# A two-layer graph network on one core: ScalarE writes the own term of six of 24 slot tiles into PSUM, and the order of tiles, engines and PSUM buffers is laid out anew

## The chip, the core and the metric

The kernel runs on one core of a Trainium2 chip. The core has TensorE (matrix products, written PE in the profile, with PEld for the loading of its weights), VectorE (DVE), ScalarE (ACT), GpSimd (POOL) and SyncE (SP), whose queue issues nearly all DMA transfers here. Products land in PSUM, a memory of eight banks of 2 KB per partition; everything else lies in SBUF. The metric is the device time of one execution in microseconds (us).

## The reference, cut to what matters

There are 128 graphs of 128 nodes with 64 features, and two layers that each add to x. The first layer is the costly one: for every node j and each of its neighbours k it applies a ReLU to 192 hidden values, and adds these up over the neighbours.

```python
# layer 0, B = N = 128, F = O = 64, H = 192
h    = maximum(layernorm(x), 0)
mask = (adj > 0)
W1a, W1b = W1[:F], W1[F:]
hid  = relu((h @ W1a)[:, :, None] + (h[:, :, None] - h[:, None, :]) @ W1b + b1)
hm   = einsum('bjkh,bjk->bjh', hid, mask)
x    = x + hm @ W2 + mask.sum(-1)[..., None] * b2
# layer 1
h    = maximum(layernorm(x), 0)
x    = x + einsum('bnm,bmf->bnf', adj, h) @ W.T
```

The hidden value of the pair (j, k) is ReLU(a_j - c_k): one term that belongs to the node j itself, the *own term*, and one that belongs to its neighbour k. A node has some 16 neighbours, so the kernel doesn't form all 128 pairs of a node.

## The kernel before, in words

The 128 graphs are worked on in 32 groups of four. The neighbours of a node are taken by quarters of 32 nodes; in each quarter the first six neighbours of every node get a *slot*. A one-hot matrix S (slot, node j) picks the neighbour's value from the table `k3` by a matmul. A neighbour that finds no slot in its quarter goes through a second, smaller path (tiles `ov`, `R`, `S2`, `px`, `X`, `pe`).

**A tile** (class `Job`) holds one graph and half of its nodes (64), and two of the quarters, `qp`: 2 x 6 slots x 64 nodes = 768 columns in two PSUM banks. There are 16 tiles of kind 0 in a group (the first 128 hidden values) and 8 of kind 1 (the other 64 hidden values of two graphs together), 24 in all, written t0 to t23 below in the order in which the group works on them. `fill` writes a tile by TensorE: for each quarter one matmul of 384 columns with S picks the neighbours (profile: `g<-S,k`), then four matmuls of 192 columns with a repeated identity, `id3`, add the own term (`g<-id,k`). In kind 1 each of these is two matmuls of half the width. The values in `k3` are split into three bf16 parts that are stacked over 96 rows, so that one product adds all three. `drain` empties the tile: kind 0 by one VectorE reduction of absolute values (`hm<-g`), since ReLU(v) = (v + |v|)/2 and the plain sum comes from elsewhere; kind 1 by a ScalarE ReLU (`T<-g`) and a tree of GpSimd additions.

**The tables of the next group** are made while a group's tiles run. `pre_proj` projects (`pp`) into PSUM; ScalarE rounds this to a first bf16 part (`ca<-pp`), VectorE takes the remainder (`rest`), ScalarE rounds a second part (`ca<-rest`), GpSimd forms the third. `pre_stack` then copies the parts by twelve SyncE transfers into `k3` (profile: `k<-ca`), four quarters for each part, part by part. Beside this, `pre_rank` and `pre_slots` make S by six VectorE comparisons (`S<-qs`), and twelve SyncE transfers spread it over three copies for each quarter (`S<-S`). SyncE's queue thus issues in each group, in this order: the twelve of S, the twelve of `k`, the store of a result, and the loads of `x` and `adj`.

**The order** is written out by hand: `ORDER` lists the tiles, and `PLAN` says after which tile which step of which group is issued; steps of the next group have 1, of the group after that 2, of the one before -1. Each engine executes in this order. `ORDER0`/`PLAN0` and `ORDERL` are for the first and the last group. PSUM is three buffers of two banks (`gtile`, for tiles and `pp`) and two of one bank (`mtile`, for everything else), taken in turn.

**The e term** is the part of the result that depends on a node alone; ScalarE scales it out of `pp` in four instructions (`e<-pp,dn`), and GpSimd adds x to it (`e<-e,x`).

Every engine instruction goes through a helper, so that the profile shows lines L181 (matmul), L184 (transpose) and L198 (the other engines) for nearly everything; the tile names tell them apart.

Of the kernel before, what the change touches and what calls it, by code (L numbers as in the profile page):

```python
# [150 lines left out]
def kernel(  # L151
# [34 lines left out]
    class Engine:  # L186


        held = True
# [38 lines left out]
    with ExitStack() as main:  # L228
# [5 lines left out]
        ps_g = main.enter_context(tc.tile_pool(name="ps_g", bufs=3, space=PSUM))  # L234
        ps_m = main.enter_context(tc.tile_pool(name="ps_m", bufs=2, space=PSUM))

        def gtile(name):
            return ps_g.tile([P, 2, 512], F32, tag="g", name=name)

        def mtile(name):  # L240
            return ps_m.tile([P, 512], F32, tag="m", name=name)
# [130 lines left out]
        def weights_d():  # L372
            pl = mtile("pl")
            tp(pl[:, 0:P], wl1, ident)
            vec.tensor_copy(wl1t, pl[:, 0:P])
# [53 lines left out]
        def pre_stats(g):  # L429
            d = groups[g]  # L430
            d["mv"] = norm_a(d["x"], f"a{g}")
# [9 lines left out]
        def norm1(g, bs):  # L441
            d = groups[g]
            for b in bs:
                normed(d["h"][:, b % 2, b // 2, :], d["x"], d["scales"], b)
# [9 lines left out]
        def norm2(g, bs):  # L454
            d = groups[g]
            for b in bs:
                normed(d["h2"][:, b, :], d["x1"], d["scales"], b)
# [12 lines left out]
        def pre_adj(g):  # L470
            d = groups[g]
            pt = mtile(f"pt{g}")
            for b in range(G):
                tp(pt[:, b * N : (b + 1) * N], d["adj"][:, b, :], ident)
            d["adjT"] = grp.tile([P, G, N], F32, tag="adjT", name=f"adjT{g}", bufs=3)
            if g == 0:
                pre_norm(0)
            act.activation(
                d["adjT"].rearrange("k b j -> k (b j)"), pt, AF.Copy
            )  # L480
            if g < 2:
                return
            pre_mask(g)

        def pre_mask(g):
            d = groups[g]
            d["maskT"] = grp.tile([P, G, N], BF16, tag="maskT", name=f"maskT{g}", bufs=3)
            vec.tensor_scalar(d["maskT"], d["adjT"], 0.0, -1.0, ALU.is_gt, ALU.mult)
            if "mv" not in d:
                pre_stats(g)  # L490
# [7 lines left out]
        def pre_rank(g):  # L498
            d = groups[g]
            pq = mtile(f"pq{g}")  # L500
            mm(
                pq, triq, d["maskT"].rearrange("k b j -> k (b j)"), start=True, stop=True
            )
            d["qs"] = grp.tile([P, G, N], BF16, tag="qs", name=f"qs{g}")
            qf = d["qs"].rearrange("k b j -> k (b j)")
            act.activation(qf, pq, AF.Copy)

            d["ov"] = grp.tile([P, G, N], BF16, tag="ov", name=f"ov{g}")
            vec.tensor_scalar(d["ov"], d["qs"], float(D) + BIG, None, ALU.is_ge)

        def pre_slots(g, first, last):

            d = groups[g]
            if first == 0:
                d["S"] = one.tile([P, D, G * N], BF16, tag="S", name=f"S{g}")
            for i in range(first, last):
                vec.tensor_scalar(
                    d["S"][:, i], d["qs"].rearrange("k b j -> k (b j)"),
                    float(i) + BIG, None, ALU.is_equal,
                )  # L520
            if last < D:
                return
# [32 lines left out]
        def pre_hT(g):  # L555
            d = groups[g]
            ph = mtile(f"ph{g}")
            for r in range(2):
# [4 lines left out]
                )  # L563
            d["hT"] = tmp.tile([P, 2, N], F32, tag="hT", name=f"hT{g}", bufs=1)
            act.activation(
                d["hT"].rearrange("p r n -> p (r n)"), ph[:, 0 : 2 * N], AF.Copy
            )

        def pre_count(g):
            d = groups[g]  # L570

            pd = mtile(f"pd{g}")
            for b in range(G):
# [5 lines left out]
                )  # L579
            d["dn"] = grp.tile([P, 2, G], F32, tag="dn", name=f"dn{g}")  # L580
# [14 lines left out]
        def pre_proj(g, r, between=None):  # L595

            d = groups[g]
            if r == 0:

                d["ca"] = grp.tile([P, 3, 2, G, H], BF16, tag="ca", name=f"ca{g}")  # L600

# [3 lines left out]
            pp = gtile(f"pp{g}_{r}")  # L605
# [8 lines left out]
            for p in range(2):  # L614
# [5 lines left out]
            x = pp[:, :, 0 : 2 * H].rearrange("n p (t u) -> n p t u", t=2)  # L620
            parts = [
                d["ca"][:, i].rearrange("n t (p r) u -> n r p t u", p=2)[:, r] for i in range(3)
            ]
            act.activation(parts[0], x, AF.Copy)
            rest = tmp.tile([P, 2, 2, H], F32, tag="rest", name=f"rest{g}_{r}")

            def zs():
                for p in range(2):
                    b = 2 * p + r
                    for to, us, f in (  # L630
                        (d["z"][:, b], slice(0, C0), AF.Abs),
                        (d["z1"][:, r, p], slice(C0, H), AF.Relu),
                    ):
                        act.activation(to, x[:, p, 1, us], f, scale=d["ns"][:, b : b + 1])


            def es():
                for p in range(2):
                    b = 2 * p + r
                    act.activation(  # L640
                        d["e"][:, b], pp[:, p, 2 * H : 2 * H + O], AF.Copy,
                        scale=d["dn"][:, 0, b : b + 1],
                    )

            def second():
                act.activation(parts[1], rest, AF.Copy)

            def third(*engines):
                for t, engine in enumerate(engines):
                    engine.tensor_tensor(  # L650
                        parts[2][:, :, t], rest[:, :, t], parts[1][:, :, t], ALU.subtract
                    )

            def add_x():
                pool.tensor_tensor(d["e"], d["e"], d["x"], ALU.add)

            def residual():
                vec.tensor_tensor(rest, x, parts[0], ALU.subtract)

            return residual, zs, es, second, third, add_x  # L660

        def project(g, r):
            d = groups[g]
            d["steps", r] = pre_proj(g, r)
            d["steps", r][1]()
            d["steps", r][2]()
            if r == 1:
                d["steps", r][5]()

        def project_rest(g, r):  # L670
            groups[g]["steps", r][0]()

        def project_parts(g, r):
            steps = groups[g].pop(("steps", r))
            steps[3]()
            steps[4](pool, pool)

        def pre_stack(g):
# [13 lines left out]
        def pre_edge_a(g):  # L692
            d = groups[g]
            pv = mtile(f"pv{g}")
            mm(pv[:, 0:G], upb, d["nb"], start=True, stop=True)
            mm(pv[:, G : 2 * G], oneb, d["nb"], start=True, stop=True)
            vec.tensor_tensor(ovf, ovf, pv[:, G : 2 * G], ALU.max)

# [4 lines left out]
        def edge_abs(g):  # L703
            d = groups[g]
            d["et"] = tmp.tile([P, G, E], F32, tag="et", name=f"et{g}", bufs=1)
            for b in range(G):
                act.activation(d["et"][:, b, :], iov, AF.Abs, bias=d["mid"][:, b : b + 1])

        def pre_place(g):

            d = groups[g]
            pj = mtile(f"pj{g}")
# [8 lines left out]
            )  # L721
            d["qj"] = tmp.tile([P, G, N], BF16, tag="qj", name=f"qj{g}", bufs=1)
            act.activation(d["qj"].rearrange("j b k -> j (b k)"), pj, AF.Copy)
# [12 lines left out]
        def pre_edge_c(g):  # L736
            d = groups[g]
            pr = mtile(f"prt{g}")
            for b in range(G):
                mm(  # L740
                    pr[:, b * N : (b + 1) * N], d["R"][:, b, :], identb, start=True, stop=True
                )
            d["RT"] = grp.tile([P, G, N], F32, tag="RT", name=f"RT{g}")
            act.activation(d["RT"].rearrange("e b j -> e (b j)"), pr, AF.Copy, scale=-1.0)

        def pre_edge_d(g):
            d = groups[g]
            pg = mtile(f"pgq{g}")
            for b in range(G):
# [3 lines left out]
                )  # L753
            d["S2"] = grp.tile([P, G, E], BF16, tag="S2", name=f"S2{g}")
            vec.tensor_tensor(
                d["S2"], pg.rearrange("k (b e) -> k b e", b=G), bc(ioe, G, 1), ALU.is_equal
            )

        def edge_x(g, r):
            d = groups[g]  # L760
            if r == 0:
                d["X"] = grp.tile([P, G, H], F32, tag="X", name=f"X{g}", bufs=1)
            px = mtile(f"px{g}_{r}")
            for p in range(2):
                b = 2 * p + r
                for t, one_hot in enumerate(("S2", "R")):
                    for i in range(3):
# [3 lines left out]
                        )  # L771
            pxv = px[:, 0 : 2 * H].rearrange("e (p u) -> e p u", p=2)
# [12 lines left out]
        def edge_sum(g):  # L785

            d = groups[g]
            ph = mtile(f"pe0{g}")
            for b in range(G):
# [5 lines left out]
                for i in range(3):  # L795
# [3 lines left out]
                    )  # L799
            d["u0"] = tmp.tile([P, G, N], F32, tag="u0", name=f"u0{g}", bufs=1)  # L800
# [4 lines left out]
        def edge_sum1(g):  # L805
            d = groups[g]
            ph = d["pe1"] = mtile(f"pe1{g}")
# [12 lines left out]
        def edge_sum2(g):  # L820
# [8 lines left out]
        def post0(g):  # L829
            d = groups[g]  # L830
            py = d["py"] = mtile(f"py{g}")
# [11 lines left out]
        def post1(g):  # L843
# [4 lines left out]
            )  # L848
            d["mv"] = norm_a(d["x1"], f"b{g}")

        def post3(g):
            d = groups[g]
            pg = mtile(f"pga{g}")
# [243 lines left out]
```

## Time and profile before

| | |
|---|---|
| median of 3 runs | 963.09 us (962.8 to 963.93) |
| the profiled execution | 964.39 us, of which 962.6 us from the first to the last instruction (the span) |
| mean granted TensorE clock | 0.994 |
| busy in the span | PE 931.3 us, DVE 770.5, POOL 739.2, ACT 685.8 |
| DMA | 129.93 MB in 88296 packets; queue 1 took 58.3% of 16 engines' span |

"Busy" counts an instruction from its start to its end; consecutive instructions of an engine overlap, so what an instruction costs its engine is the distance to the start of the next one, which the timeline shows. In groups of instructions, `out<-in` names the tiles, with the numbers of buffers left out: `S<-S` is the transfer from the one-hot matrix to its copies.

### The profile page before, as it was taken

The numbers are of one execution on the slowest core, as the hardware profiler recorded it, in microseconds if no ns is written. First come the engines' busy times: TensorE is split into PE (matmuls) and PEld (weight loads), VectorE is DVE, ScalarE is ACT, GpSimd is POOL, SyncE is SP. The second block draws the span as 40 slices with busy tenths as digits, with TensorE's granted clock in tenths as the row PEclk, the third lists the DMA queues.
The fourth block names the chain that finished last, engine by engine and source line by source line (L and its number), as shares of the span: only waits on it lengthen the run. The fifth ranks groups of instructions, "written<-read, shape, count | busy, mean of one in ns | idle before, by whom it ended". The sixth has DMA issues, their size and how long they took to land.

```text
span 962.6 us, 27044 instructions
## 1 busy us (share of the span) xinstructions
PE 931.3 (97%) x10135; PEld 715.1 (74%) x10136; DVE 770.5 (80%) x1880; ACT 685.8 (71%) x1700; POOL 739.2 (77%) x1130
## 2 busy tenths in 40 slices
PE   6899999999999999999999999999999999999996
PEld 2677777777777777777777777777777777777774
DVE  6787878887878887878887878887878888878864
ACT  4857787767787767787767787667787667787652
POOL 1488787778787778787778787778887778887793
PEclk9999999999999999999999999999999999999998
DMA  4555676655576655676655576655676655676510
GB/s 101 127 126 128 142 165 146 147 130 127 142 171 140 142 134 127 142 170 141 146 130 128 140 171 140 142 133 123 146 163 144 148 129 129 142 172 140 125 46 14
DMA packets 88296, 129.93 MB, mean 135 GB/s; under 512 B 47200, under 2 KB 63968, under 8 KB 88160
## 3 DMA queue, kind: packets, MB, share of 16 engines
q1 hardware_dynamic: 87584, 127.98, 58.3%
q8 instruction: 82, 1.34, 0.6%
q14 instruction: 54, 0.44, 0.1%
q10 hardware_dynamic: 576, 0.16, 0.1%
HBM read 13.01 MB, written 4.19 MB: 18 GB/s over the span
## 4 chain that ended last, share of the span: by engine, by line
PE 68%; DVE 15%; ACT 10%; DMA 4%; POOL 1%; issue 1%; SPq 0%; POOLq 0%; ACTq 0%; DVEq 0%
PE g L181 39%; PE pe L181 9%; PE px L181 6%; DVE hm L198 5%; ACT z L198 3%; ACT ca L198 3%; DVE rest L198 3%; DMA S<-S 3%; PE pp L181 2%; DVE stb L198 2%; PE po L181 2%; ACT e L198 1%; DVE u L198 1%; PE pga L181 1%; PE ph L184 1%; PE pj L181 1%
## 5 line engine op out<-in xcount | busy, mean ns | idle before, releaser
L198 POOL TENSOR_TENSOR T<-T 128x192 f32<-128x192 f32 (+2 forms) x768 | 522.6, 687 | 119.1 <-ACT T L198 79.2
L198 DVE TENSOR_REDUCE hm<-g 128x64 f32<-128x768 f32 x512 | 477.1, 948 | 100.9 <-PE g L181 96.1
L181 PEld LDWEIGHTS <-k 96*128 96x128 bf16 (+1 forms) x6144 | 413.1, 104 | 173.7 <-issue 55.4
L181 PE MATMUL g<-S,k 96*128 96x384 bf16 (+1 forms) x2048 | 381.7, 329 | 12.3 <-DVE hm L198 10.2
L181 PE MATMUL g<-id,k 96*128 96x192 bf16 (+1 forms) x4096 | 380.0, 246 | 0.0
L198 ACT ACTIVATE T<-g 128x768 f32<-128x768 f32 x256 | 206.0, 819 | 73.5 <-PE g L181 69.6
L198 POOL TENSOR_TENSOR ca<-rest,ca 128x384 bf16<-128x384 f32 x126 | 112.4, 912 | 77.8 <-ACT ca L198 43.1
L198 ACT ACTIVATE ca<-pp 128x768 bf16<-128x768 f32 x64 | 51.3, 801 | 52.8 <-PE pp L181 33.5
L198 ACT ACTIVATE ca<-rest 128x768 bf16<-128x768 f32 x64 | 55.1, 861 | 31.0 <-DVE rest L198 31.0
L198 DVE TENSOR_TENSOR rest<-pp,ca 128x768 f32<-128x768 f32 x64 | 60.8, 950 | 15.2 <-ACT e L198 14.8
L181 PE MATMUL pe<-RT,X 128*64 128x128 f32 (+1 forms) x512 | 70.5, 280 | 0.0
L181 PE MATMUL pp<-wp,hT 64*128 64x448 f32 x256 | 67.0, 601 | 0.4 <-DVE bias L198 0.4
L198 ACT ACTIVATE z<-pp,ns 128x128 f32<-128x128 f32 (+1 forms) x256 | 65.7, 346 | 0.0
L198 ACT ACTIVATE qs<-pq 128x512 bf16<-128x512 f32 x32 | 19.1, 597 | 54.4 <-PE pq L181 52.6
L198 ACT ACTIVATE et<-et,half 128x128 f32<-128x128 f32 x128 | 57.0, 449 | 0.0
L181 PEld LDWEIGHTS pe<-RT,X 128*64 128x64 f32 (+1 forms) x512 | 52.7, 165 | 5.4 <-issue 5.4
L181 PE MATMUL px<-ca,S 128*128 128x192 bf16 x384 | 52.7, 246 | 0.0
L181 PE MATMUL px<-ca,R 128*128 128x192 bf16 x384 | 52.6, 246 | 0.0
L198 ACT ACTIVATE h<-x,mrb,rsb 128x64 f32<-128x64 f32 x128 | 51.5, 477 | 0.5 <-DVE mrb L198 0.5
L198 ACT ACTIVATE h<-x,mra,rsa 128x64 f32<-128x64 f32 x128 | 48.6, 432 | 1.8 <-issue 1.3
L198 POOL TENSOR_TENSOR hm<-T 128x64 f32<-128x64 f32 x128 | 40.8, 318 | 9.9
L181 PE MATMUL pe<-ident,z 128*128 128x128 f32 x192 | 48.0, 277 | 0.0
(125 smaller groups left out, 1216.3 us busy)
## 6 DMA issues: line engine op xcount, KB each, us to landing
S<-S SPq DMA_DIRECT2D x372, 192.0 KB, 4.0
k<-ca SPq DMA_DIRECT2D x384, 96.0 KB, 2.2
adj<-in_adj_dram SPq DMA_DIRECT2D x32, 256.0 KB, 3.2
x<-in_x_dram SPq DMA_DIRECT2D x32, 128.0 KB, 2.9
out_dram<-ot SPq DMA_DIRECT2D x32, 128.0 KB, 2.2
w<-in_L_gnn_W_dram SPq DMA_DIRECT2D x2, 96.0 KB, 4.3
bias<-in_L_gnn_b_dram ACTq DMA_DIRECT2D x1, 96.0 KB, 3.6
w2a<-in_L_gnn_W_dram ACTq DMA_DIRECT2D x1, 32.0 KB, 2.2
```

Source lines behind the costliest of these rows:

```text
L181: return tc.keep_in_program_order(nc.tensor.matmul(*args, **kw))
L184: return tc.keep_in_program_order(nc.tensor.transpose(*args, **kw))
L198: ins = f(*args, **kw)
```

## The change

Six of the 24 tiles of a group (kind 0: t0, t2, t3, t7, t8 and t20, of graphs 0 and 2 of the group) no longer get their own term from the four `g<-id,k` matmuls. Instead

- TensorE forms the own term once in a group for these graphs, by six matmuls with an identity into one PSUM bank (`own_pe`, tile `pa`);
- VectorE copies it to SBUF by two instructions (`own_dve`, tile `at`);
- ScalarE writes it, repeated over 2 x 6 slots, into the tile's two PSUM banks (`seed`, one instruction of 768 columns), and the two S matmuls then add to it, with `start=False`.

This holds in groups 1 to 30; `own_pe` and `own_dve` run for groups 1 to 31. The four `e<-pp,dn` instructions of ScalarE and the addition of x on GpSimd become four VectorE instructions (`pp_e`), which multiply and add at once. The order of the tiles is new, the steps are cut finer (the TensorE part and the engine that empties its result are placed apart), `PLAN` is written anew, and in groups 1 to 30 the PSUM buffer of each tile and step is fixed by the table `BANKS`. `adjT` and `maskT` have four buffers in place of three.

```diff
+        def own_pe(g):
+            d = groups[g]
+            pa = d["pa"] = mtile(f"pa{g}", "own_pe")
+            for n, (b, jhs) in enumerate(OWN):
+                o = slice(n * N + jhs[0] * JH, n * N + jhs[-1] * JH + JH)
+                for i in range(3):
+                    mm(
+                        pa[:, o], d["ca"][:, i, 1, b, 0:C0],
+                        identb[:, jhs[0] * JH : jhs[-1] * JH + JH], start=i == 0, stop=i == 2,
+                    )
+
+        def own_dve(g):
+            d = groups[g]
+            d["at"] = grp.tile([P, len(OWN), N], F32, tag="at", name=f"at{g}")
+            for n, (b, jhs) in enumerate(OWN):
+                o = slice(jhs[0] * JH, jhs[-1] * JH + JH)
+                vec.tensor_copy(d["at"][:, n, o], d["pa"][:, n * N + o.start : n * N + o.stop])
...
+        def pp_e(g, r):
...
+                vec.scalar_tensor_tensor(
+                    d["e"][:, b], d["pp", r][:, p, 2 * H : 2 * H + O], d["dn"][:, 0, b : b + 1],
+                    d["x"][:, b], ALU.mult, ALU.add,
+                )
...
         class Job:
+            def seed(self):
+                self.seeded = True
+                n = [b for b, _ in OWN].index(self.b)
+                own = groups[self.g]["at"][:, n, self.jh * JH : (self.jh + 1) * JH]
+                act.activation(
+                    self.gt[:, :, 0:ND].rearrange("h i (d j) -> h i d j", d=D),
+                    bc(bc(own, D, 1), 2, 1), AF.Copy,
+                )
             def fill(self):
...
-                            start=True, stop=False, skip_group_check=True,
+                            start=not self.seeded, stop=self.seeded, skip_group_check=True,
+                if self.seeded:
+                    return
...
+        OWN = ((0, (0, 1)), (2, (1,)))
...
+            0: "over|1",
+            1: "sum0_pe|-1 seed|0 sum0_dve|-1 norm1|1|2 norm1|1|0 slot|1|0 hT_pe|1",
+            2: "seed|0 load|2",
+            3: "count_pe|1 hT_act|1 slot|1|1 slot|1|2 sum1_pe|-1",
+            4: "count_dve|1 slot|1|3",
+            5: "sum1_dve|-1 pp_pe|1|0 seed|1 slot|1|4 pp_e|1|0 edge_pe|1 slot|1|5 edge_dve|1",
+            6: (
+                "pp_ca|1|0 edge_abs|1|0 edge_abs|1|1 seed|1 x_pe|0|0 edge_abs|1|2 edge_relu|1|1 "
+                "pp_rest|1|0"
+            ),
+            7: "pp_z|1|0 y_pe|-1 x1_dve|-1",
+            8: "x_act|0|0",
+            9: "stats_a|2 stats_b|-1",
+            10: "edge_relu|1|0 pp_second|1|0",
+            11: "root_b|-1 edge_abs|1|3",
+            12: "slots_dma|1 scale_b|-1 edge_relu|1|2 pp_pe|1|1 pp_z|1|1 pp_ca|1|1",
+            13: "root_a|2 norm2|-1|3 x_pe|0|1 place_pe|1 norm2|-1|2 pp_rest|1|1 place_act|1 pp_e|1|1",
+            14: "pp_second|1|1 pp_third|1|0 pp_third|1|1",
+            15: "norm2|-1|0 norm2|-1|1 edge_relu|1|3",
+            16: "x_act|0|1 scale_a|2",
+            17: "stack|1 seed|2 agg_pe|-1",
+            18: "own_pe|1 own_dve|1",
+            19: "agg_act|-1",
+            20: "adj_pe|2 edge_rows|1",
+            21: "adj_act|2 norm1|2|1 seed|2 out_pe|-1 turn_pe|1 slot_sum|0 mask|2 turn_act|1",
+            22: "out_dve|-1",
+            23: "find_pe|1 rank_pe|2 rank_act|2 find_dve|1 norm1|2|3",
...
+        BANKS = {
+            0: 2, 1: 1, 2: 0, 3: 2, 4: 1, 5: 0, 6: 0, 7: 1, 8: 0, 9: 1, 10: 2, 11: 0, 12: 1,
+            13: 0, 14: 1, 15: 0, 16: 2, 17: 1, 18: 0, 19: 1, 20: 2, 21: 0, 22: 1, 23: 0,
+            "adj_pe": 1, "agg_pe": 0, "count_pe": 1, "edge_pe": 1, "find_pe": 1, "hT_pe": 0,
+            "out_pe": 0, "own_pe": 1, "place_pe": 0, "pp_pe|0": 2, "pp_pe|1": 2, "rank_pe":
+            0, "sum0_pe": 1, "sum1_pe": 0, "turn_pe": 1, "x_pe|0": 0, "x_pe|1": 1, "y_pe": 1,
+        }
...
+        ORDER = [
+            (0, 0, 0, 0), (0, 3, 0, 1), (0, 0, 0, 1), (0, 0, 1, 0),
+            (1, 0, 0, 1), (1, 1, 1, 1), (0, 2, 0, 1), (0, 2, 1, 1),
+            (0, 2, 1, 0), (1, 0, 0, 0), (1, 0, 1, 1), (0, 3, 1, 1),
+            (0, 1, 1, 0), (0, 3, 0, 0), (0, 1, 0, 1), (0, 1, 1, 1),
+            (0, 2, 0, 0), (1, 0, 1, 0), (1, 1, 1, 0), (0, 3, 1, 0),
+            (0, 0, 1, 1), (0, 1, 0, 0), (1, 1, 0, 1), (1, 1, 0, 0),
+        ]
```

An entry of `ORDER` is (kind, graph or pair, half of the nodes, `qp`). `seed|n` after a tile writes the own term of the tile n + 1 places later. The steps' names are those of before cut in two: `sum0` is the old `edge_sum` (`pe`, `u`), `sum1` the old `edge_sum1`/`edge_sum2`, `x` the old `edge_x` (`px`, `X`), `y`/`x1` the old `post0`/`post1`, `agg` and `out` the old `post3` and `post4`, `stack` the old `pre_stack`, `slot` and `slots_dma` the old `pre_slots`.

## The prediction

> **What bounds the kernel now.** I read the page first, then the waits, then timelines of a middle group.
>
> ```profile
> PE 931.3 (97%) x10135; PEld 715.1 (74%) x10136; DVE 770.5 (80%) x1880; ACT 685.8 (71%) x1700; POOL 739.2 (77%) x1130
> ...
> q8 instruction: 82, 1.34, 0.6%
> ...
> S<-S SPq DMA_DIRECT2D x372, 192.0 KB, 4.0
> k<-ca SPq DMA_DIRECT2D x384, 96.0 KB, 2.2
> ```
>
> TensorE looks like the bound. The waits agree, but their last two lines name a second clock: SyncE's queue rests only 232.5/31 = 7.5 us in a group, waiting for S, and TensorE now and then meets a `k` table that has just landed.
>
> ```profile
> DVE hm L198 <- PE g L181: 96.1, 97, 2.1
> ...
> PE g L181 <- DVE hm L198: 10.2, 31, 2.9
> ...
> SPq L198 <- DVE S L198: 232.5, 31, 9.4
> ...
> PEld L181 <- DMA k<-ca: 1.4, 7, 0.3
> ```
>
> TensorE's timeline around the start of a group (t0 at 487.64, t1 at 488.73):
>
> ```profile
> 487.40 0.40 PE L181 MATMUL pgq<-R,qj 128*128 128x128 bf16 x4
> 487.64 0.49 PE L181 MATMUL g<-S,k 96*128 96x384 bf16 x2
> 487.96 0.49 PE L181 MATMUL g<-id,k 96*128 96x192 bf16 x4
> 488.29 0.60 PE L184 MATMUL pt<-ident,adj 128*128 128x128 f32 x4
> 488.73 0.50 PE L181 MATMUL g<-S,k 96*128 96x384 bf16 x2
> ...
> 489.73 0.33 PE L181 MATMUL pe<-maskT,ca 128*128 128x128 bf16 x3
> 489.90 0.28 PE L181 MATMUL pe<-ident,z 128*128 128x128 f32 x1
> ```
>
> From start to start, the two S matmuls cost 0.32 us, the four `id` matmuls 0.33 (487.96 to 488.29), three of 128 columns 0.17. SyncE's queue in the same group, first S, first `k`, last `k`:
>
> ```profile
> 495.89 0.51 SPq L198 DMA_DIRECT2D S<-S  x1
> ...
> 506.23 0.77 SPq L198 DMA_DIRECT2D k<-ca  x1
> ...
> 514.64 0.59 SPq L198 DMA_DIRECT2D k<-ca  x1
> ```
>
> With 2.2 us to land, the last `k` is there at 516.8; the next t0 started at 516.49 and t1, which reads the last quarters, at 517.59. So before, the queue already ends about where TensorE needs it. The chain that ended last shows it too, in two groups:
>
> ```profile
> 599.07 4.12 DMA k<-ca
> ...
> 657.67 3.85 DMA k<-ca
> ```
>
> **The sum for TensorE, if nothing else binds.** First S issues lie 28.89 us apart (63.07 to 900.93, 29 groups). In a middle group the starts sum to 27.8 us of matmuls and some 1.1 us of waits. Removed: 6 tiles x 0.33 = 2.0 us. Added: `own_pe`, three of 128 columns (0.17) and three of 64 (at most as much): 0.35. Left: 26.2 us of work.
>
> **The other engines**, by their rests in 480 to 508.86. ScalarE works 21.3 us of a group; `e` leaves (four, two in 0.39 us: -0.8). A write by ScalarE into PSUM is nowhere in this trace. Nearest rows of 768 columns: `T<-g` from PSUM to SBUF, 0.70 us from start to start, and `ca<-rest` from SBUF, 0.74. I take 0.74, since the seed reads SBUF too; ends 0.6 and 1.1 (0.74 and half again, for a repeated source and a new destination). Six make 4.4: ScalarE 24.9 (24.1 to 27.1). VectorE works 23.7; `own_dve` 0.33 and four `e` of 0.17 (between the 0.07 of `half<-pd` and the 0.34 of `x<-py,e`) add 1.0: 24.7. GpSimd loses 0.7 of 23.1. The additional buffers cost nothing. I then went through the new order by hand with these distances, adding 0.05 us from an end to the waiting start: the seeds of t2, t7, t8 and t20 are done before TensorE arrives; that of t3 makes it wait 0.1 to 0.2, `hm` of t14 0.2 at t17, `adjT` 0.15 at `prt`. That alone gives about 26.7 us a group.
>
> A clock gate is the rule that speaks against this: before, the granted clock was 1.00 in every stretch of 30 us from 60 to 930, with waits of TensorE up to 2.9 us. The Trainium skill, "TensorE: Matmul & The Clock Gate", section "A second HAM failure mode: psum-queue depth-cycling", says that short idle times between groups which cycle through PSUM can make the clock swing between half and full. By that rule a tenth of the group at half clock would add some 2.6 us (estimate) and eat the whole gain; I go by the row.
>
> **What is late next: SyncE's queue.** The change takes no transfer away. Its loop is: t1 starts, S is compared, S and `k` are issued, `k` lands, the next t1 starts. Its parts in the new order, from t1's start: t1 0.66 and `pe` 2.03, complete at 2.85; VectorE then does `u` (0.66, to 3.55), one comparison (0.23), `hm` of t2 and t3 (0.87 each), two comparisons, the four count steps (0.48), a comparison, the second `u` (0.33), a comparison: 7.25. Two `e` wait here for `pp`: TensorE reaches its end at 7.2 over `ph` 0.25, t2 and t3 0.66, `pd` 0.3, `pe` 0.8, t4 and t5 1.44, `pp` 1.07. The `e` and the sixth comparison bring 7.9, the first S issue 8.0. Before it was 495.89 - 488.73 = 7.2, counted from t0 8.25.
>
> From the first S to the first `k` the queue took 10.34 us, in nearly every group; the DMA share is 0.99 to 1.03 from 498 to 506, so the twelve S are bound by the transfers and stay. From there to the last `k` 8.2 in an undisturbed group (18.51 in all), of which the fifth `k` waits for ScalarE's second part: "SPq <- ACT X" has 33.2 us in 27 waits, 1.2 each. In the new order, gone through as above, that part is done some 11 us after the first S, before the queue gets there; of the 1.2 I take 0.7 as saved (0 to 1.2), as the queue needs its own 0.6 for an issue. So the last `k` is issued at 17.8 and lands at 20.0; t1's second matmul reads it, 0.16 after the first.
>
> Two edits tighten this. t0 is seeded, 0.33 in place of 0.65, and `pt` no longer stands between t0 and t1: t1 comes 0.33 after t0, not 1.09. And S is ready 0.8 later against t1. The loop: 8.0 + 20.0 - 0.16 + 0.05 = 27.9 us. It is longer than 26.7, so it decides: new waits of TensorE for `k` at t1.
>
> Disturbed groups: before, every second group's late `k` transfers landed 1 to 1.5 us later. The one at 599.07 needed 4.12 in place of 2.2, the trace's packets have an instruction fetch of 16 KB for 1.66 us at 600.40 on the same engines, and this group lasted 29.3 us. There were five such fetches in two groups, always at the same places. TensorE has 633 instructions a group, in future 597, so some 2.35 fetches that drift; about 4 us of 27.9 are vulnerable, a third of the groups. Take 1.1 for a hit: 27.9 + 0.4 = 28.3. The gain is 0.6 x 30 groups = 18 us: 964.4 - 18 = 946 for the profiled execution, 945 for the median, which lay 1.3 below it. Group 0, the last group and the tail keep their work.
>
> Other moves on the queues: the issue of S now stands after t12 and that of `k` after t17 in the program, but SyncE waits only for their data, and its order is unchanged. The loads behind the store start 1 us into the group, and `pt` needs them 20 us later. On GpSimd both third parts stand behind the T of t10 and end 12.5 us after the first S, 3 before the ninth `k`; behind them wait the T of t17 and t18, with 3 us to spare.
>
> **Rivals.**
>
> *The queue gives way* (0.14). If S and `k` go faster once they start elsewhere, TensorE with its new waits sets 26.7 to 27.4: 964 - 30 x 1.5 to 2.2 = 898 to 919. For it: k issues of 0.51 us exist. Against: 10.34 us for S at a full DMA share.
>
> *The sixth comparison comes later, slower than before* (0.25). Place: VectorE's `e` and last S comparison, behind `pp`. Each us there adds one to the loop, 30 us in all; as the loop with its disturbances is 28.3, it decides from 0.6 us. A seed of 1.1 us, late for t3, or fetches that hit two groups in three would do. At 1.2 us: 29.5, 964 + 18 = 982.
>
> *ScalarE becomes the bound.* Going through the order leaves it 1.9 us without work before the T of t4; 20.5 (21.3 - 0.8) + 1.9 + 6s exceeds 28.9 from s = 1.08. That is part of the case before.
>
> *The matmuls aren't saved*: the built program has 1068 fewer TensorE rows, 30 x 48 - 31 x 12, so excluded.
>
> **How the numbers follow.** About 0.2% (2 us) is what a measurement of this kernel can tell from no change. Forecast, 27.6 to 28.7 a group (925 to 959): 0.54, faster. Queue gives way: 0.14, faster. A loop of 28.9, with the time within 2 us: 0.07, same. A longer loop: 0.25, slower. So faster 0.68, same 0.07, slower 0.25. The range, 912 to 974, leaves out most of the first rival and the worse half of the second.
>
> **What would show it.** Right: TensorE's wait "PE g or PEld <- DMA k" grows from 2 us to 30 or more, at t1; busy PE falls by some 48 us (30 x 1.6) while the span falls by 18; SyncE's rest for S shrinks below 7.5 us; a seed takes 0.7 to 0.8 us. Wrong: first S less than 7.5 us after t1, or the last `k` landing within 19 us of the first S (then 900 to 920); TensorE waiting most for ScalarE or VectorE; a clock below 0.95.

## The result, and the profile after

The changed kernel takes 1013.43 us (median; 1011.21 to 1013.98) beside 963.51 us before: a ratio of 1.0514, 95% interval 1.0496 to 1.0532. It is slower by 50 us; forecast were 945, with 974 as the upper end. The profiled execution took 1013.98 us, its span is 1012.2.

The page of the changed kernel: busy times, TensorE's granted clock in 40 slices, SyncE's transfers, and the shares of the chain that ended last.

```profile
PE 928.9 (92%) x9601; PEld 705.5 (70%) x9602; DVE 821.7 (81%) x2070; ACT 778.9 (77%) x1752; POOL 718.1 (71%) x1098
...
PEclk9798999999999999999999999999999999999997
...
PE 23%; POOL 21%; SPq 16%; DMA 14%; DVE 11%; ACT 9%; issue 5%; POOLq 0%; DVEq 0%; ACTq 0%
...
S<-S SPq DMA_DIRECT2D x372, 192.0 KB, 4.1
k<-ca SPq DMA_DIRECT2D x384, 96.0 KB, 2.2
```

TensorE went from 97 to 92% busy. Its 534 removed matmuls show only as 2.4 us less busy time, where some 48 were expected: the others took longer. The transfers land as fast as before. TensorE heads the chain with only 23%; GpSimd, SyncE and the transfers together have 51.

The waits of the changed kernel:

```profile
DVE hm L198 <- PE g L181: 64.4, 85, 3.5
...
PEld L181 <- DMA k<-ca: 38.7, 60, 1.9
PE g L181 <- DMA k<-ca: 34.7, 84, 1.8
...
PE g L181 <- DVE hm L198: 4.5, 7, 2.8
PE g L181 <- ACT g L198: 2.2, 9, 0.4
...
SPq L198 <- DVE S L198: 290.8, 34, 10.7
```

The two rows of `k` are partly the same waits, seen once by the weight loads and once by the matmuls, and can't be added. Counted once, they are 51.8 us, against 1.7 before: SyncE's loop sets the group, as forecast. TensorE waits 2.2 us for seeds, so these are in time. But SyncE's rest for S, forecast to shrink, grew from 232.5 to 290.8 us: S is ready later.

TensorE's timeline around t0 and t1 of a middle group, and from the chain the `pe` behind them, first in a group of the kernel before, then in this group:

```profile
486.73 0.34 PE L181 MATMUL g<-S,k 96*128 96x384 bf16 x1 [0.26 <-DMA k<-ca]
487.42 0.34 PE L181 MATMUL g<-S,k 96*128 96x384 bf16 x1 [0.35 <-DMA k<-ca]
488.04 0.34 PE L181 MATMUL g<-S,k 96*128 96x384 bf16 x1 [0.29 <-DMA k<-ca]
488.84 0.33 PE L181 MATMUL g<-S,k 96*128 96x384 bf16 x1 [0.46 <-DMA k<-ca]
```

```profile
200.85 2.02 PE pe L181 x24
```

```profile
489.81 3.33 PE pe L181 x24
```

Four matmuls that take 0.16 us each from start to start last from 486.73 to 489.00: 2.27 us, 1.6 of them standing still, one wait for each transfer. Then `pe` takes 3.33 us, 2.02 before. The windows, with the granted clock in the third column from the end, show why; the second stretch is another part of the same run:

```profile
480.00:510.00 30.00, 28.55 (x296) 21.96 (x293) 24.57 (x64) 24.02 (x56) 22.15 (x35) 0.94 0.58 135
570.00:600.00 30.00, 28.51 (x307) 21.25 (x305) 27.05 (x65) 25.20 (x57) 23.22 (x36) 1.00 0.62 143
```

The clock's own records say it exactly: between 60 and 930 us it falls to 0.5 nineteen times, for 71.7 us in all, mostly 3.413 us at a time (at 489.02, 519.74, 550.46: 30.72 apart, nine times 3.413). Before there was no such stretch there. All nineteen begin within 1.1 us of the landing of a last `k`. In 29 of the groups 1 to 30 TensorE's matmuls wait three or four times in a row there; the group shown has only short waits, in others one of them lasts up to 2.0 us. In the second window, with much the same waits, the clock held.

The second loss is on VectorE. First the comparisons S as a group on the page before, then after, then in the timeline after GpSimd's additions for T and a comparison beside them:

```profile
L198 DVE TENSOR_SCALAR S<-qs 128x512 bf16<-128x512 bf16 x186 | 45.4, 297 | 0.0
```

```profile
L198 DVE TENSOR_SCALAR S<-qs 128x512 bf16<-128x512 bf16 x186 | 74.1, 414 | 0.1
```

```profile
586.32 3.34 POOL L198 TENSOR_TENSOR T<-T 128x384 f32<-128x384 f32 x4 [1.07 <-ACT T L198]
...
586.39 1.07 DVE L198 TENSOR_SCALAR S<-qs 128x512 bf16<-128x512 bf16 x1
```

The mean went from 297 to 414 ns. Sorted by what GpSimd did meanwhile, the 103 comparisons with GpSimd at rest for most of their time take 295 ns at most, and the 83 beside it 575 on average, 1087 at most. Before, 50 lay beside it. What counts is the start: the 108 comparisons that start while no GpSimd instruction runs take 295 ns at most, and of the 78 that start inside one, 72 end 0.15 us after that instruction, however long it still takes. The order by hand moved the comparisons into GpSimd's work on T; six in a group now take 0.7 us longer than before.

Both losses lie in one place. From the records of issue and landing, means over the 28 groups from the third first S to the last (the kernels from the fourth on are experiments, below):

| kernel | first S to last `k` landed | last `k` landed to next first S | group |
|---|---|---|---|
| before | 21.22 | 7.68 | 28.89 |
| forecast | 20.4 | 7.9 | 28.3 |
| after | 20.67 | 9.56 | 30.23 |
| seven idle matmuls | 20.53 | 8.57 | 29.10 |
| no seeds | 20.61 | 8.97 | 29.58 |
| before, four more transfers | 23.26 | 7.06 | 30.31 |
| two comparisons early | 22.42 | 5.83 | 28.24 |

From the first S of group 2 to that of the last group the kernel lost 41.0 us. Outside of this, group 0 lost 7.9 us (first S of group 1 to first S of group 2: 37.8 us, before 29.8) and the tail 2.5, and the first S of all came 1.8 us earlier. Together this makes 49.6 us, the difference of the two spans.

### The profile page after: what moved, and what is told of

Same layout as the page of the kernel before. It is cut to its first block, busy times and chain, and to the rows that moved or that the text cites. A ratio compares the mean times of both kernels' runs of the same rounds, so it can differ in the third digit from the quotient of the medians.

```text
span 1012.2 us, 26312 instructions
## 1 busy us (share of the span) xinstructions
PE 928.9 (92%) x9601; PEld 705.5 (70%) x9602; DVE 821.7 (81%) x2070; ACT 778.9 (77%) x1752; POOL 718.1 (71%) x1098
## 4 chain that ended last, share of the span: by engine, by line
PE 23%; POOL 21%; SPq 16%; DMA 14%; DVE 11%; ACT 9%; issue 5%; POOLq 0%; DVEq 0%; ACTq 0%
SPq L198 16%; POOL T L198 11%; PE pe L181 10%; POOL ca L198 9%; PE g L181 8%; DMA S<-S 7%; DMA k<-ca 7%; DVE S L198 4%; DVE hm L198 4%; ACT ca L198 2%; PE pp L181 2%; ACT et L198 2%; ACT z L198 2%; ACT T L198 1%; ACT g L198 1%
## 5 line engine op out<-in xcount | busy, mean ns | idle before, releaser
L181 PEld LDWEIGHTS <-k 96*64 96x64 bf16 (+1 forms) x5424 | 365.6, 105 | 206.0 <-issue 86.8
L181 PE MATMUL g<-id,k 96*64 96x192 bf16 (+1 forms) x3376 | 300.5, 248 | 0.0
L198 ACT ACTIVATE g<-at 128x768 f32<-128x768 f32 x180 | 148.2, 823 | 9.9 <-DVE hm L198 9.6
L181 PE MATMUL pe<-RT,X 128*64 128x128 f32 (+1 forms) x512 | 85.3, 314 | 0.0
L198 ACT ACTIVATE hT<-ph 128x256 f32<-128x256 f32 x32 | 12.3, 384 | 88.2 <-PE ph L184 88.2
L198 DVE TENSOR_SCALAR S<-qs 128x512 bf16<-128x512 bf16 x186 | 74.1, 414 | 0.1
L198 DVE TENSOR_TENSOR u<-hs,pe 128x512 f32<-128x512 f32 x32 | 22.0, 688 | 64.1 <-PE pe L181 52.4
L181 PEld LDWEIGHTS pe<-RT,X 128*64 128x64 f32 (+1 forms) x512 | 67.5, 198 | 5.4 <-issue 5.4
L181 PE MATMUL pe<-ident,z 128*128 128x128 f32 x192 | 57.7, 328 | 0.0
L181 PEld LDWEIGHTS <-ca 128*128 128x128 bf16 x570 | 51.2, 114 | 8.9
```

The lines of the kernel that those rows point to most:

```text
L181: return tc.keep_in_program_order(nc.tensor.matmul(*args, **kw))
L198: ins = f(*args, **kw)
```

## The experiments

The theory (Q): SyncE's loop sets the group, and its length is S ready plus issues. Rivals: the seeds themselves (S in the expectations), the order of the steps (O), the clock, the collision on VectorE. All but the last run are single executions, beside 960.8 to 964.0 us for the kernel before on the same chip, so differences of 2 or 3 us between runs say little.

### Four more transfers in the kernel before

```diff
+            if g:
+                extra = one.tile([QN, 4, 2 * H], BF16, tag="extra", name=f"extra{g}")
+                for i in range(4):
+                    sp.dma_start(
+                        extra[:, i], d["ca"][0:QN, 0, 0, 0:2].rearrange("n b u -> n (b u)")
+                    )
```

> The kernel before, with four additional small SyncE transfers (32 x 768 bytes into an unused tile) between S and k in groups 1 to 31. Theory Q says that the queue already ends where TensorE needs k: four issues of 0.55 to 0.65 us, of which up to 0.7 hides in the fifth k's wait for ScalarE, make a group 1.5 to 2.3 us longer, and the new waits at t0 and t1 bring the clock down, for another 0 to 1.5: 1005 to 1070. If the queue has slack (rivals S, O): 963 to 968.

1010.47 us, near the lower end. The small transfers stand between S and `k`, and from the first S to the landing of the last `k` it takes 2.0 us longer; the group grew by 1.4 us, a little less than the 1.5 to 2.3 expected. TensorE's wait is the one of the changed kernel (waits):

```profile
PEld L181 <- DMA k<-ca: 25.3, 45, 1.2
```

So the loop had little slack in the kernel before either: 0.6 of the 2.0 us. This confirms the step of the prediction on which all rests. The clock, though, fell only twice in mid-run here: a wait for `k` doesn't bring it down by itself.

### Seven idle matmuls at t0 and t1

```diff
+                if t < 2 and 1 <= g < NG - 1:
+                    keep_busy(job(g, 1).gt[:, 0], 4 if t == 0 else 3)
```

> The changed kernel with seven needless matmuls of 512 columns in each of groups 1 to 30, four ahead of t0 and three between t0 and t1, into t1's buffer, which t1 then overwrites: TensorE is kept at work while it waits for k. Theory Q with the clock as its second part: the granted clock stays at 1.00 in most groups (mean over 0.98), a group falls from 30.3 to 29.1 us, the time to 970 to 985. If the low clock is not caused by these waits, or costs nothing on the way that counts: 1010 to 1045, as 1.5 us of work a group come on top.

980.33 us, 33 less than the changed kernel, with more work for TensorE. Window of this kernel:

```profile
480.00:510.00 30.00, 29.90 (x318) 22.60 (x317) 26.75 (x66) 25.23 (x57) 22.98 (x35) 1.00 0.62 143
```

The clock has no low stretch between 48 and 965 us. From the last `k` to the next S is 8.57 in place of 9.56 us: the clock costs 1 us a group there. In the records 0.9 of it lies in `pe`, which takes 3.09 us on average from its first start to its last end in the changed kernel, and 2.19 with the idle matmuls, as before the change. What remains against the forecast, 8.57 to 7.9, lies mostly between the end of `u` and the end of the sixth comparison: 4.92 us on average, where the prediction's walk has 4.35 (from 3.55 to 7.9).

### No seeds

```diff
+                    if name in ("own_pe", "own_dve", "seed"):
+                        continue
```

> The changed kernel without the six ScalarE seeds, without own_pe and own_dve; all 24 tiles get their own term from the matmuls again, in the new order and with the new buffers. Theory Q (SyncE's queue sets the group: S compared, S and k issued, k landed, t1; and TensorE's waits there bring its clock down): the 1.6 us of matmuls come back into TensorE's waits, so the time stays near 1013, 995 to 1015, and TensorE still waits for k at t1 (over 40 us in all). Rival S (the seeds: ScalarE's writes into PSUM and what is queued behind them cost the time): back to 960 to 970. Rival O (the order of the steps inside the engines makes other waits than those for k): 1030 to 1060, as 1.6 us a group come on top.

991.4 us, just below the range of theory Q and outside those of the rivals; the rows of waits for `k` have 23.6 us (matmuls) and 26.4 (weight loads). Without its very purpose the change is faster by 22 us, and still 27 slower than before. Where the loop binds, a seed saves nothing: it makes t0 shorter, TensorE waits instead, and the clock falls (three low stretches here in mid-run, nineteen with the seeds). But the seeds aren't the whole loss; the order laid out by hand has its own.

### All six comparisons at t0

```diff
-            0: "over|1",
+            0: "over|1 slot|1|0 slot|1|1 slot|1|2 slot|1|3 slot|1|4 slot|1|5 slots_dma|1",
```

(and their later places emptied)

> The changed kernel with VectorE's six S comparisons moved right behind ov at t0 (before: strewn from t1 to t5), and the twelve S transfers issued first in the group, ahead of the loads. Nothing else moves. Theory Q: the first S is issued some 3.5 us after t0 instead of 9 to 10; k is then bound by its third parts on GpSimd and lands about 26 us after t0, so the queue stops setting the group; the engines do, with 27 to 28 us, the clock stays near 1.00, and the time falls to 915 to 945. Rivals S and O: no gain, 1005 to 1030, since VectorE's reductions come later behind the comparisons.

1154.25 us, a miss by over 200. VectorE's timeline, and GpSimd's beside it:

```profile
512.99 3.83 DVE L198 TENSOR_SCALAR S<-qs 128x512 bf16<-128x512 bf16 x6
...
513.61 4.71 POOL L198 TENSOR_TENSOR T<-T 128x384 f32<-128x384 f32 x6
```

Six in a row beside GpSimd take 3.83 us; six in a row in group 0 of the kernel before, at 31.90, took 1.29. They push back `hm` of t1 and `u`: TensorE then waits 71.8 us for `hm` and 91.7 for `u`. The loads of the next group, now queued behind S, make VectorE wait 77.6 us. The mean clock fell to 0.902 as well, and what part of the loss is the clock's isn't separated. The loop can't be shortened by pushing everything else aside.

### The comparisons spread, with and without seeds, with and without idle matmuls

```diff
-            0: "over|1",
-            1: "sum0_pe|-1 seed|0 sum0_dve|-1 norm1|1|2 norm1|1|0 slot|1|0 hT_pe|1",
-            2: "seed|0 load|2",
+            0: "load|2 over|1 slot|1|0",
+            1: "sum0_pe|-1 seed|0 slot|1|1 slot|1|2 slot|1|3 sum0_dve|-1 slot|1|4 slot|1|5 slots_dma|1 norm1|1|2 norm1|1|0 hT_pe|1",
+            2: "seed|0",
```

(and the later places of the comparisons emptied)

> The changed kernel, but VectorE makes the comparisons S from t0 on in the rest that it has there before the sums at t1 (first S right behind the tile's overflow step, the sixth right behind the means of t1), and the next group's loads are issued by SyncE ahead of the S transfers. Theory Q (SyncE's loop t1, S, k, t1 sets the group's length): first S about 5 us after t0's wait, so 4 us earlier, and the loop falls below TensorE's own work; 27.0 to 28.5 us a group, 925 to 960 us, TensorE's waits for k in the small and gone in most groups, its clock at 1.00 in mid-run. If the loop isn't what binds (rival: seeds or VectorE's load), 1000 to 1030 us. A miss like that of the six comparisons at t0 (VectorE's work for t1 pushed back) would show as waits of TensorE for u or g of VectorE and 1040 us or more.

> The comparisons spread as in the spread version, and no seeds: the own term of all tiles by TensorE and VectorE again as before the change. If the matmuls and additions that the seeds save are worth something once the loop doesn't bind, this is 1.0 to 1.6 us a group slower than the spread version (30 to 48 us); if the loop still binds in both, the two are equal or this one is up to 20 us faster, as it was without the spread (991.4 against 1013).

> The spread version plus the seven idle matmuls at t0 and t1. If TensorE no longer waits for k there, the idle matmuls cost their own 1.5 us a group and the time is that of the spread version plus 0 to 45 us; if it still waits and its clock falls, this one is faster by up to 33 us, as it was with the changed kernel's own order.

986.65 us with seeds, 984.39 without, 982.77 with seeds and idle matmuls; a group takes 29.2 to 29.3 us in all three. With seeds, S is ready earlier (6.27 us from the last `k`) and the rows of waits for `k` have 8.6 and 6.9 us, but the time is above the range, and the clock still falls eleven times in mid-run, for 44 us; in the other two it doesn't. What is late now is `u`, behind three comparisons that take 0.3, 0.7 and 1.1 us on average (waits of the spread version):

```profile
PE pd L181 <- DVE u L198: 49.1, 30, 2.1
```

The loop was relieved and VectorE's `u` took its place; seeds are worth nothing there either.

### Less for GpSimd

```diff
-                for n in (D, D // 2):
+                bare = Engine.planned and (b, jh) == (1, 0)
+                for n in () if bare else (D, D // 2):
```

(and two of the three last additions of these tiles)

> The kernel with the seven idle matmuls at t0 and t1 (980.3 us, 29.1 us a group), but in groups 1 to 30 GpSimd leaves out all but the last of its additions of T for the two tiles beside which the comparisons S run; that part of the sum is missing. Theory V (the comparisons are stretched because GpSimd adds T at the same time): mean of one comparison 414 down to about 300 ns, first S 0.7 us earlier or more, and with the loop binding 28.4 us a group, 957 to 964 us. Without the collision as cause: 414 ns stays, 975 to 982 us.

979.58 us against 980.33: no difference. The mean of a comparison fell only from 418 to 388 ns, since the additions that stand beside the fifth and sixth comparison belong to other tiles. By place the run says more: the first and the fourth comparison, beside which additions are left out, fell from 400 and 416 ns to 286 and 282; the fifth and sixth went from 747 and 418 to 857 and 360. Together the six are 0.2 us shorter, and from the last `k` to the next S it is 8.37 in place of 8.57 us. So where GpSimd's additions go, the stretch goes; what all of it is worth in time, this run doesn't show.

### Two comparisons early, four behind `u`

```diff
-            1: "sum0_pe|-1 seed|0 slot|1|1 slot|1|2 slot|1|3 sum0_dve|-1 slot|1|4 slot|1|5 slots_dma|1 ...
+            1: "sum0_pe|-1 seed|0 slot|1|1 sum0_dve|-1 slot|1|2 slot|1|3 slot|1|4 slot|1|5 slots_dma|1 ...
```

(against the spread version; both lines cut at their end)

> The spread version with only two comparisons ahead of the first u (one behind the overflow step at t0, one in VectorE's rest behind it) and the other four behind u. Theory Q (SyncE's loop, as long as nothing else is late): u comes 1.2 us earlier than in the spread version, TensorE's wait for u (49 us in all there) all but goes, S is complete 0.6 us later, which its loop of about 26 us still bears: 27.2 to 28.2 us a group, 935 to 965 us, clock above 0.98. If VectorE as a whole is what binds now (rival V: 27.8 us of its work in a group of 28.6), the wait only moves to its later work and the time stays at 978 to 988 us.

> The version with two comparisons early, without the seeds: every own term by TensorE and VectorE as before the change. If TensorE is the bound there, it is 1.0 to 1.6 us a group (30 to 48 us) slower than the version with the seeds; if VectorE or the loop binds, the two lie within 10 us.

953.29 us with seeds, 970.87 without. VectorE's timeline of the version with seeds, and its waits:

```profile
488.82 0.28 DVE L198 TENSOR_SCALAR S<-qs 128x512 bf16<-128x512 bf16 x1
489.78 0.69 DVE L198 TENSOR_TENSOR u<-hs,pe 128x512 f32<-128x512 f32 x1 [0.68 <-PE pe L181]
490.39 1.29 DVE L198 TENSOR_SCALAR S<-qs 128x512 bf16<-128x512 bf16 x4
```

```profile
PE g L181 <- DVE hm L198: 26.9, 31, 2.8
...
PEld L181 <- DMA k<-ca: 10.1, 20, 1.4
```

`u` is again limited by `pe`, S is complete at 491.7, and in mid-run the clock falls once, for 3.4 us. 26 of the 28 groups last 28.2 us: the loop no longer decides. Here the seeds are worth 17.6 us, 28.8 to 28.2 a group. That is 0.6, between the two expectations (1.0 to 1.6 us a group, or within 10 us in all): VectorE is busy 26.2 of 28.2 us, and TensorE now waits 0.9 us a group for `hm`. That VectorE takes the rest is argued from these rows, not shown by a run.

### Group 0

```diff
+                if (g, t) == (0, 10):
+                    keep_busy(mtile("keep0"), 6)
```

(added to the version with two comparisons early)

> The version with two comparisons early, plus six idle matmuls on TensorE in group 0 where it waits 2.3 us for the PSUM buffer that pp holds. If the half clock behind that wait is what makes group 0 long, first S of group 1 to first S of group 2 falls from 36 to 38 us to 31 to 33 us and the time by about 4 us; if the order of VectorE's work is the reason, it stays within 1 us.

In the changed kernel's timeline t10 of group 0 waits behind `e` and `rest`, which on VectorE now stand in a row ahead of `mid`:

```profile
39.01 0.85 PE L181 MATMUL g<-S,k 96*64 96x384 bf16 x4 [2.35 <-DVE mid L198]
```

From 38.46 the clock was low for 10.2 us. In the version with two comparisons early the same happens. With six idle matmuls in this place it stays at 1.00 from 34 to 65 us (0.85 without them, from 34 to 68), and first S of group 1 to first S of group 2 falls from 34.5 to 30.7 us; the time is 950.24, 3 us less. The low clock behind that one wait costs about 4 us there.

> The version with two comparisons early and the idle matmuls of group 0 once more, timed against the kernel before. One execution gave 950.2 us against 960.8 us; if that holds, the ratio is 0.985 to 0.992 with an interval wholly below 1, 948 to 954 us. If the single look was luck, the interval takes in 1.

The same kernel, timed several times: 951.8 us (951.24 to 952.82) beside 964.69 before, ratio 0.9873, interval 0.9856 to 0.9889. This version as a whole is 1.3% faster than the kernel before. The seeds have their part in it: without them, two comparisons early gave 970.87 us, 10 above the kernel before.

## Why the prediction was wrong

*TensorE's own sum.* Right as to the count. That the matmuls removed aren't seen as time is what "late next" said. The sum of 26.7 us a group was never reached: the best version stands at 28.2, and what holds it there isn't shown.

*ScalarE's seed.* 0.74 was forecast, mostly 0.73 to 0.75 us from start to start were measured where the next instruction didn't wait, and TensorE waits 2.2 us in all for seeds. ScalarE as the bound is refuted:

```profile
L198 ACT ACTIVATE g<-at 128x768 f32<-128x768 f32 x180 | 148.2, 823 | 9.9 <-DVE hm L198 9.6
```

Two `e` on VectorE take 0.39 us, where 0.34 was taken.

*SyncE's loop becomes the bound.* Right, by the waits for `k` and by the four added transfers.

*From the first S to the last `k`.* 20.0 undisturbed and 20.4 with disturbances forecast; 19.8 at the least and 20.67 on average measured. Nearly right. *The queue gives way* is refuted: no group came below 19.8, and the sign named for it was 19.

*From the landing of `k` to the next S.* This is the term that failed: 7.9 us forecast (8.0 - 0.16 + 0.05), 9.56 measured, 1.7 x 30 = 50 us. It has two parts. First, 0.7 us: each comparison was put at 0.23 us from start to start, as it goes without GpSimd, and the walk along the new order never asked what GpSimd does at that moment. The stretch itself is shown by the rows and by the two comparisons that lost it; that it makes all of the 0.7 is argued from their sizes. Second, 1.0 us, shown by the idle matmuls: "I go by the row" on the clock. The rows of before had single waits, but the forecast itself made new ones, and they came as three or four waits in a row at the start of nearly every group, which no row of before showed. The mean clock, 0.949, is just below the 0.95 that the prediction named as a sign against it. The rule set aside had the right direction, but its estimate of 2.6 us a group was more than twice the price of 1.0. The same page of the Trainium skill, "TensorE: Matmul & The Clock Gate", has a nearer case in the section "HAM oscillation — how this bites in real kernels": waits for transfers, repeated at every step, throttle TensorE each time, but there each wait is 3 to 5 us long. Here no wait at the nineteen places was longer than 2.0 us, and at four of them none was longer than 0.5.

*The sixth comparison comes later.* This rival had the right term of the loop and the right sign, and a chance of 0.25. Its cause was wrong (VectorE didn't wait for `pp`; the comparisons themselves became longer, and `pe` ahead of them), and its price too small: 1.2 us was taken, 1.7 it was.

*Group 0 keeps its work.* It kept its work and lost 8 us: a step put at nothing without its row. The low clock behind one wait accounts for about 4, by the six idle matmuls; the changed order on VectorE stands ahead of that wait, and the other 4 aren't separated.

Added up from the forecast of 946: 0.7 x 30 = 21 for the comparisons, 1.0 x 30 = 30 for the clock, 0.27 x 30 = 8 for the way from the first S to the last `k`, 7.9 in group 0 and 2.5 in the tail, less the 1.8 at the start, give 1014; the profiled execution took 1014.

## What to carry to other kernels

When a change lets another loop overtake TensorE, cost that loop with the engine that now waits in it: new short waits of TensorE in a row can halve its clock, and then the loop grows with it. Before work is removed from the bound engine, move the late step of the next loop: here the same seeds cost 22 us with S late and gained 18 with S early. When an order is laid out by hand, look at what the neighbour engine does beside each moved instruction, not only at what it waits for.

## What the runs showed of the hardware

A VectorE comparison of 128x512 bf16 takes 0.28 us, and up to 1.09 beside GpSimd's additions in f32, yet not beside all of them. In the records it depends on which of the two starts first. With all six at t0, 119 comparisons start while a GpSimd instruction runs, and every one of them ends 0.15 us after that instruction (0.149 to 0.157); the other 67 take 0.28 us. Of the four at 490.39 above, three take 0.28 us, and the one that starts inside an addition takes 0.68. The changed kernel has three exceptions in 78, which start inside an addition and still take 0.29 us. The Trainium skill, "Advanced Engine Details and Errata", section "VectorE Performance Modes", says that VectorE's second port is shared with GpSimd, so that instructions which use both ports and GpSimd's hold each other up; the rows agree for the side of VectorE.

The clock falls in pieces of 3.413 us or multiples of it, on a fixed grid: within a run their starts in mid-run lie whole multiples of it apart. Some 1.6 us of waits in 2.3 us were enough at 486.73; at 577.98, with 1.5 in 2.1, the clock held, so what decides between such cases isn't shown. Idle matmuls in the waits kept it up, and 33 us were gained by work that computes nothing.
